# A two-layer graph network on one core: first layer's sums kept in SBUF, three PSUM banks of totals, a longer way out, and the second layer's way out in another order

## The chip, the cores and the metric

The kernel runs on one core of a Trainium2 chip. The metric is the device time of one execution in microseconds (us), the median over several runs. The engines are named as in the profile: PE (TensorE, matrix products), DVE (VectorE), ACT (ScalarE), POOL (GpSimd), SP (SyncE, which here only starts DMAs). SBUF is the on-chip memory, PSUM the banks into which PE writes.

## The reference

There are 6250 nodes with 256 features, 200000 edges sorted by their target `dst`, and 128 attributes on each edge. Two layers follow each other, each with a residual and a layer norm. Cut to what matters:

```python
# layer 1
e   = edge_attr @ W_edge + b_edge
msg = relu(x[src] + e)
agg = segment_sum(msg, dst, num_segments=N)
h   = (1.0 + eps) * x + agg
h   = relu(h @ W1 + b1) @ W2 + b2
h   = relu(batch_norm(h))             # mean and variance over the nodes
x   = layernorm(x + h)
# layer 2: four heads of 64
z   = einsum('nd,hdf->nhf', x, W)
e   = leaky_relu(es[src] + ed[dst])   # es, ed: z times the halves of att
ex  = exp(e - segment_max(e, dst)[dst])
out = segment_sum(ex / segment_sum(ex, dst)[dst] * z[src], dst)
x   = layernorm(x + out)
```

## The kernel before

The edges are cut into 1563 subtiles of 128. Fourteen subtiles make a group (112 groups), and two neighbouring subtiles make a pair (7 pairs in a group, 782 in all). The targets of a group's edges lie in a window of 128 nodes, so a segment sum over a group is a series of products with one-hot matrices, added up in one PSUM bank. A node whose edges run over a group's end gets a carry from one group to the next.

**Layer 1** takes from the start to about 2300 us. Its loop (from L728) runs over the pairs k. The steps are:

- `fetch(k+3)` (L645) issues on POOL two indirect DMAs, the gathers, each of 128 rows of x (with the edge bias added) by `src`, into a buffer `xg` (128x512, 11 buffers, in SBUF).
- `features(k+3)` (L653 and L655) multiplies on PE the edge attributes by W_edge into a PSUM bank `pt` (5 banks).
- `sums(k)` (L659, DVE) adds `xg` to `pt`, in `pt`; `xg` is free after it.
- `upper(k)` (L664, ACT) takes the relu of `pt`, rounded to the products' type, into one half of `hl`; `lower(k-1)` (L668, DVE) writes what the rounding lost, max(pt, 0) minus the upper half, into the other half. `pt` is free after it.
- `add_up(k-2)` (L678, PE) adds the pair into the group's bank `acc` by one-hots that ACT makes (L621, L627).

Four pairs after a group's last one, `flush` starts: `totals` adds the node's own x on DVE (L514, L515), transposes on PE (L518), copies on ACT (L520) and applies the carry on DVE (L523 to L531); for every second group `mlp` runs the two products for two groups (L408, L416; the relu r1 at L412 and the copy h2 at L424 on ACT), and `part_stats` (L431 to L440) adds to the batch norm's statistics. These are generators: a step yields the number of pairs to wait before its next step, and `drive` in the loop calls them.

**Between the layers**, from about 2300 to 2480 us, the batch norm, the residual, the layer norm and the tables of z are worked out.

**Layer 2** runs over groups i. POOL gathers 14 times 128 rows of z into `ring` (L1003; 70 places of one subtile, five groups). `places` (L1034, L1037, ACT) makes the transposed one-hots from `dlb`, which SP loads; PE takes from them the targets' part of the logits (L1054); `logits` (L1083 to L1087, then scans at L1072 and L1076) and `maxima` (L1119 to L1131) give the exponents on DVE and ACT; `weigh` multiplies them with the gathered z on DVE (y, L1140) and adds up on PE (acc, L1144) by one-hots of ACT (L1061, L1067). `carry` and `leave` take a group out: ACT copies the last group's carried row pc to pcs (L1151), DVE scales it (cr, L1153) and adds it to acc (L1155), ACT copies acc to ag (L1158), PE takes the next carried row from it (pc, L1160), and `finish_steps` (L371 to L389) divides, adds the residual and normalises; SP stores the result `o` (L1171).

The order of the work on DVE, PE, ACT and SP is the order in which the program lists it (a manual schedule); each engine works its list off in order and waits where an operand or a buffer is not ready. POOL's queue holds practically only the gathers, and it waits only for a free buffer. In `fetch` the wait is for a `xg` buffer, in layer 2 for a place of `ring`, which y frees.

Of the kernel before, what the change touches and what calls it, by code (L numbers as in the profile page):

```python
# [54 lines left out]
def gnn(ctx, tc, io, N, E):  # L55
# [345 lines left out]
    def mlp(hw, h2_dst, pool, pps, parts_=(None,)):  # L401

        w = len(parts_) * P
        p1 = pps.tile([P, 2, w], F32, tag="pt", name="p1")
        r1 = pool.tile([P, 2, w], F32, tag="r1", name="r1", bufs=1)
        for m in range(2):
            for k in range(2):
                nc.tensor.matmul(p1[:, m, :], w1_sb[:, k, m * P:(m + 1) * P], hw[:, k, :w],  # L408
                                 start=(k == 0), stop=(k == 1))
            yield 1 if m == 0 else 4  # L410
        for m in range(2):
            nc.scalar.activation(r1[:, m, :], p1[:, m, :], AF.Relu, bias=b1_c[:, m:m + 1])  # L412
        p2 = pps.tile([P, 2, w], F32, tag="pt", name="p2")
        for m in range(2):
            for k in range(2):
                nc.tensor.matmul(p2[:, m, :], w2_sb[:, k, m * P:(m + 1) * P], r1[:, k, :],  # L416
                                 start=(k == 0), stop=(k == 1))
            yield 1 if m == 0 else 4
        for i, part in enumerate(parts_):
            if i:  # L420
                yield 1
            cols_ = slice(i * P, (i + 1) * P)
            for m in range(2):
                nc.scalar.activation(h2_dst(m, i), p2[:, m, cols_], AF.Identity, bias=b2_c[:, m:m + 1])  # L424
            if part is not None:
                part(p2[:, :, cols_])
# [72 lines left out]
    with ExitStack() as st:  # L499
# [5 lines left out]
        pe = st.enter_context(tc.tile_pool(name="pe", bufs=5, space=PSUM))  # L505
        pg = st.enter_context(tc.tile_pool(name="pg", bufs=2, space=PSUM))
# [4 lines left out]
        def totals(g, acc, xw, hw):  # L511

            ag = wk.tile([P, D], F32, tag="ag", name="ag")
            nc.vector.scalar_tensor_tensor(ag, xw, opem[:, g:g + 1], acc[:, 1], op0=OP.mult, op1=OP.add)  # L514
            nc.vector.tensor_add(ag, ag, acc[:, 0])  # L515
            pT = acc[:, 0].rearrange("p (k n) -> p k n", k=2)
            for k in range(2):
                nc.tensor.transpose(pT[:, k, :], ag[:, k * P:(k + 1) * P], ident)  # L518
            yield 3
            nc.scalar.copy(hw, pT)  # L520
            old = carried[0]
            if old is not None:
                nc.vector.tensor_add(hw[:, :, 0], hw[:, :, 0], old)  # L523
            if g + 1 < G:
                end = nc.values_load(span_i[:1, g:g + 1], engines=[ET.DVE], min_val=0, max_val=P - 1,
                                     skip_runtime_bounds_check_because="the value is clamped")
                new = wk.tile([P, 2], F32, tag="carry", name="carry")
                nc.vector.tensor_scalar(new, pT[:, :, ds(end, 1)].rearrange("p k o -> p (k o)"), keep0[:, g:g + 1],  # L528
                                        None, op0=OP.mult)
                if old is not None:  # L530
                    nc.vector.scalar_tensor_tensor(new, old, whole0[:, g:g + 1], new, op0=OP.mult, op1=OP.add)  # L531
                carried[0] = new


        HW = {}

        def flush(g, acc, xw):

            two = G - G % 2 - 2
            if g < two and g % 2 == 0:  # L540
                HW[g + 1] = wk.tile([P, 2, 2 * P], F32, tag="hw", name="hw")
                yield from totals(g, acc, xw, HW[g + 1][:, :, :P])
                return
            hw = HW.pop(g, None)
            if hw is None:
                hw = wk.tile([P, 2, P], F32, tag="hw", name="hw1")
                yield from totals(g, acc, xw, hw)
                both = [g]
            else:
                yield from totals(g, acc, xw, hw[:, :, P:])  # L550
                both = [g - 1, g]
            yield -1
            bases = [nc.values_load(gf_i[:1, q:q + 1], engines=[ET.Activation], min_val=0, max_val=N - 1,
                                    skip_runtime_bounds_check_because=IN_RANGE) for q in both]
            yield from mlp(hw, lambda m, i: h2T[:, m, ds(bases[i], P)], wk, pps, [part_stats(q, wk) for q in both])
            if len(both) > 1:
                room[0] = 3
# [99 lines left out]
        def sums(k):  # L657
            g, j0, w = pairs_[k]
            nc.vector.tensor_add(PT[k][:, :w], PT[k][:, :w], XG.pop(k)[:, :w])  # L659

        def upper(k):
            g, j0, w = pairs_[k]
            HL[k] = hlp.tile([P, 2, 2, D], F32R, tag="hl", name="hl")
            nc.scalar.activation(HL[k][:, :w, 0], PT[k][:, :w], AF.Relu)  # L664

        def lower(k):
            g, j0, w = pairs_[k]
            nc.vector.scalar_tensor_tensor(HL[k][:, :w, 1], PT.pop(k)[:, :w], 0.0, HL[k][:, :w, 0].bitcast(F32),  # L668
# [17 lines left out]
        with tc.manual_schedule(engines={ET.DVE, ET.PE, ET.Activation, ET.SP}):  # L686
# [16 lines left out]
            hots, active, extras, room = iter(()), [], [], [0]  # L703
# [24 lines left out]
            for k in range(K + 2):  # L728
                g = pairs_[min(k, K - 1)][0]
                hurry = g >= G - 2  # L730
# [233 lines left out]
    with ExitStack() as st:  # L964
# [182 lines left out]
        def carry(g):  # L1147
            acc = T["acc", g]
            if g > 0:
                pcs = wk.tile([1, ZW], F32, tag="pcs", name="pcs")  # L1150
                nc.scalar.copy(pcs, T.pop(("pc", g - 1)))  # L1151
                cr = wk.tile([1, H, F + 1], F32, tag="cr", name="cr")
                nc.vector.tensor_tensor(cr, pcs.rearrange("p (h f) -> p h f", f=F + 1),  # L1153
                                        T.pop(("dm", g)).unsqueeze(2).to_broadcast([1, H, F + 1]), op=OP.mult)
                nc.vector.tensor_add(acc[:1], acc[:1], cr)  # L1155
            if g + 1 < G:
                ag = wk.tile([P, H, F + 1], F32, tag="ag2", name="ag2", bufs=2)
                nc.scalar.copy(ag, acc)  # L1158
                pc = T["pc", g] = ps.tile([1, ZW], F32, tag="pc", name="pc")
                nc.tensor.matmul(pc, ohlast[:, g:g + 1], ag.rearrange("p h f -> p (h f)"), start=True, stop=True)  # L1160

        def leave(g):
            px = rows_of(T.pop(("hw", g)), ps, "px")
            yield
            carry(g)
            o = wk.tile([P, D], F32, tag="o", name="o")
            yield from finish_steps(o, T.pop(("acc", g)), px, T.pop(("edw", g))[:, EW - 1:], wk)
# [33 lines left out]
        with tc.manual_schedule(engines={ET.DVE, ET.PE, ET.Activation, ET.SP}):  # L1201
# [10 lines left out]
            for i in range(G + 2):  # L1212
# [17 lines left out]
                if i + 1 < G:  # L1230
                    breaks(i + 1)
# [7 lines left out]
                if i == G - 1 and i > turn + 1:  # L1239
# [12 lines left out]
                    step(out)  # L1252
                    step(out)
# [3 lines left out]
                while out:  # L1257
                    step(out)
                step(outs)
                some(1, False)  # L1260
                step(spots)
                step(spots)
                for g in among([i - 1] if i <= turn else []):
                    rows_between(g)
                if i < G:
                    logits(i)
                some(1)
                step(hots)
# [4 lines left out]
                step(hots)  # L1273
                for g in among([i] if i >= turn else []):
                    rows_between(g)
                some(1)
# [3 lines left out]
                step(hots)  # L1280
                while outs:
                    step(outs)
                while units or hots:
                    some(1)
                    step(hots)
                for _ in parts_:
# [218 lines left out]
```

## Time and profile before

| | |
|---|---|
| median of 11 runs | 4953.35 us (4938.56 to 4963.66) |
| the profiled execution | 4952.23 us, span 4950.4 us |
| mean granted TensorE clock | 0.775 |
| busy: PE, DVE, ACT, POOL | 3059.7, 2699.4, 2632.4, 2968.1 us |
| gathers of layer 1: L645 | 1451 (and 112 from the first groups), mean 945 ns |
| gathers of layer 2: L1003 | 1563, mean 946 ns |
| `sums` L659, `upper` L664, `lower` L668 | 782 each, mean 691, 591, 679 ns |
| y L1140 | 782, mean 682 ns |
| 100 to 2000 us: PE, DVE, ACT, POOL busy | 1279.86, 1063.17, 1021.62, 1188.23 us |
| 2500 to 4800 us: PE, DVE, ACT, POOL busy | 1308.71, 1212.87, 1225.05, 1433.30 us |

The page gives for each group of instructions its line, engine, operation, the tiles written and read, the number, the total and mean duration, and the idle time of its engine just before it with what ended that idle time. "issue" means that the profile shows nothing that was waited for; "remote" means that the releaser is an event that the trace does not tie to an instruction. The operations of DVE and ACT are pipelined: the next one can start somewhat before the last one's end.

### The profile page before, as it was taken

The numbers are of one execution on the slowest core, as the hardware profiler recorded it, in microseconds if no ns is written. First come the engines' busy times: TensorE is split into PE (matmuls) and PEld (weight loads), VectorE is DVE, ScalarE is ACT, GpSimd is POOL, SyncE is SP. The second block draws the span as 40 slices with busy tenths as digits, with TensorE's granted clock in tenths as the row PEclk, the third lists the DMA queues.
The fourth block names the chain that finished last, engine by engine and source line by source line (L and its number), as shares of the span: only waits on it lengthen the run. The fifth ranks groups of instructions, "written<-read, shape, count | busy, mean of one in ns | idle before, by whom it ended". The sixth has DMA issues, their size and how long they took to land. (4 is left out here: it accounts for less than half of the span.)

```text
span 4950.4 us, 48894 instructions
## 1 busy us (share of the span) xinstructions
PE 3059.7 (62%) x11779; PEld 2181.6 (44%) x11779; DVE 2699.4 (55%) x7579; ACT 2632.4 (53%) x6723; POOL 2968.1 (60%) x3132
## 2 busy tenths in 40 slices
PE   6766666666666766666715655565656566555555
PEld 3545545555555555555603333333433333333343
DVE  5655555555555555555615555555555555555555
ACT  4555555555555555555525555555555555555554
POOL 7666566666666666666065666666666666666661
PEclk9888888888888888888857777777777767777777
DMA  7544444444444444444544444444444444444441
GB/s 255 163 140 139 130 137 141 139 139 140 130 139 137 142 137 140 139 140 131 154 128 115 122 126 125 120 125 126 122 117 127 126 122 126 119 124 126 128 122 42
DMA packets 296689, 656.22 MB, mean 133 GB/s; under 512 B 87274, under 2 KB 158553, under 8 KB 296394
## 3 DMA queue, kind: packets, MB, share of 16 engines
q0 software_dynamic: 150144, 416.54, 29.7%
q1 hardware_dynamic: 144650, 235.43, 14.9%
q8 instruction: 97, 1.59, 0.1%
q14 instruction: 198, 1.62, 0.1%
q10 hardware_dynamic: 1600, 1.04, 0.1%
HBM read 617.82 MB, written 34.99 MB: 132 GB/s over the span
## 5 line engine op out<-in xcount | busy, mean ns | idle before, releaser
L1003 POOL DMA_INDIRECT ring<-z_tab,src_sb x1563 | 1479.3, 946 | 1018.3 <-issue 422.0
L645 POOL DMA_INDIRECT xg<-xb_tab,src_sb x1451 | 1371.8, 945 | 822.3 <-DVE pt L659 409.6
L1144 PE MATMUL acc<-y,oh 128*128 128x260 f32 x3126 | 1173.1, 512 | 451.2 <-issue 333.8
L655 PE MATMUL pt<-we_sb,ea_t 128*128 128x256 f32 x3126 | 967.7, 439 | 244.1 <-DVE hl L668 203.6
L1144 PEld LDWEIGHTS acc<-y,oh 128*128 128x128 f32 x3126 | 701.1, 247 | 704.4 <-issue 416.6
L664 ACT ACTIVATE hl<-pt 128x512 fp32r<-128x512 f32 x782 | 462.4, 591 | 948.8 <-DVE pt L659 823.0
L659 DVE TENSOR_TENSOR pt<-pt,xg 128x512 f32<-128x512 f32 x782 | 540.5, 691 | 645.3 <-remote 534.5
L655 PEld LDWEIGHTS pt<-we_sb,ea_t 128*128 128x128 f32 x3126 | 662.2, 220 | 423.7 <-issue 262.5
L678 PE MATMUL acc<-hl,oh 128*128 128x512 f32 x1563 | 720.3, 544 | 35.8 <-DVE carry L528 17.6
L1140 DVE TENSOR_TENSOR y<-ring,exs 128x520 f32<-128x520 f32 x782 | 514.5, 682 | 60.5 <-issue 23.3
L668 DVE SCALAR_TENSOR_TENSOR hl<-pt,hl 128x512 fp32r<-128x512 f32 x782 | 530.7, 679 | 2.2 <-issue 0.9
L621 ACT ACTIVATE oh<-consts,dloc 128x128 fp32r<-128x128 f32 x1549 | 508.5, 394 | 0.0
L1061 ACT ACTIVATE oh<-consts,dloc 128x128 f32<-128x128 f32 x1563 | 480.4, 388 | 0.7 <-remote 0.7
L1034 ACT ACTIVATE ohT<-dlb,niota 128x1792 bf16<-128x1792 bf16 x112 | 199.7, 1783 | 354.9 <-DMA dlb<-dl_tab 173.7
L678 PEld LDWEIGHTS acc<-hl,oh 128*128 128x128 f32 x1563 | 339.4, 219 | 107.7 <-issue 39.3
L416 PE MATMUL p<-r,w_sb 128*128 128x256 f32 (+1 forms) x456 | 162.7, 491 | 286.3 <-ACT r L412 267.1
L1054 PEld LDWEIGHTS <-ohT 128*128 128x128 bf16 x1563 | 159.1, 113 | 357.3 <-issue 273.6
L1054 PE MATMUL pds<-edw,ohT 128*128 128x12 bf16 x1563 | 155.3, 177 | 190.6 <-issue 166.7
L416 PEld LDWEIGHTS p<-r,w_sb 128*128 128x128 f32 x456 | 108.7, 252 | 326.3 <-ACT r L412 283.5
L1153 DVE TENSOR_TENSOR cr<-pcs,dm 1x260 f32<-1x260 f32 x111 | 46.6, 419 | 374.8 <-ACT pcs L1151 189.2
L1067 ACT ACTIVATE oh<-oh 128x896 f32<-128x896 f32 x224 | 208.7, 932 | 7.8 <-remote 7.8
L627 ACT ACTIVATE oh<-oh 128x896 fp32r<-128x896 f32 (+1 forms) x222 | 209.1, 942 | 0.0
(226 smaller groups left out, 3086.1 us busy)
## 6 DMA issues: line engine op xcount, KB each, us to landing
ea_t<-in_eaT SPq DMA_DIRECT2D x110, 896.0 KB
dlb<-dl_tab SPq DMA_DIRECT2D x111, 448.0 KB
ring<-z_tab,src_sb POOLq DMA_INDIRECT x1563
xg<-xb_tab,src_sb POOLq DMA_INDIRECT x1451
xw<-in_x SPq DMA_DIRECT2D x112, 128.0 KB
hw<-hT_tab SPq DMA_DIRECT2D x112, 128.0 KB
out<-o SPq DMA_DIRECT2D x110, 128.0 KB
z_tab<-zt SPq DMA_DIRECT2D x11, 528.0 KB
```

Source lines behind the costliest of these rows:

```text
L621: nc.scalar.activation(oh[:, i], iota_r, AF.Square, bias=dloc[:, gs[g] + i:gs[g] + i + 1], scale=-1.0)
L645: nc.gpsimd.indirect_dma_start(out=XG[k][:, i, :], out_offset=None, in_=io["x"] if g < GB else xb_tab, in_offset=bass.IndirectOffsetOnAxis ...
L655: nc.tensor.matmul(pt[:, i, :], EA.pop(gs[g] + j0 + i), we_sb, start=not g < GB, stop=(not g < GB or i == w - 1))
L659: nc.vector.tensor_add(PT[k][:, :w], PT[k][:, :w], XG.pop(k)[:, :w])
L664: nc.scalar.activation(HL[k][:, :w, 0], PT[k][:, :w], AF.Relu)
L668: nc.vector.scalar_tensor_tensor(HL[k][:, :w, 1], PT.pop(k)[:, :w], 0.0, HL[k][:, :w, 0].bitcast(F32), op0=OP.max, op1=OP.subtract)
L678: nc.tensor.matmul(ACC[g].rearrange("p a d -> p (a d)"), OH[g][:, j0 + i], hl[:, i].rearrange("p a d -> p (a d)"), start=(j0 + i == 0), st ...
L1003: nc.gpsimd.indirect_dma_start(out=zg[:, j, :], out_offset=None, in_=z_tab, in_offset=bass.IndirectOffsetOnAxis(ap=src_sb[:, t:t + 1], axi ...
L1054: nc.tensor.matmul(pd[:, j].rearrange("p h c -> p (h c)"), ohT[:, j * P:(j + 1) * P], T["edw", g].bitcast(BF16)[:, :3 * H], start=True, st ...
L1061: nc.scalar.activation(oh[:, i], iota_r, AF.Square, bias=dloc[:, gs[g] + i:gs[g] + i + 1], scale=-1.0)
L1140: nc.vector.tensor_tensor(y[:, :w], T["zg", g][:, j0:j0 + w, :ZW].rearrange("p s (h f) -> p s h f", f=F + 1), by_edge(T["ex", g], g)[:, j0 ...
L1144: nc.tensor.matmul(T["acc", g].rearrange("p h f -> p (h f)"), T["oh", g][:, j0 + i, :], y[:, i].rearrange("p h f -> p (h f)"), start=(j0 + ...
```

## The change

In words:

- `sums` writes its result into `xg` (SBUF) instead of `pt` (PSUM). `pt` is free after `sums`, and `xg` only after `lower`. `upper` and `lower` read `xg`.
- There are 4 banks of products (`pe`) instead of 5, and 3 banks of totals (`pg`) instead of 2.
- In `totals` three pairs lie between DVE's sum and PE's transposes, four before ACT's copy and one before the carry. In `mlp` three pairs lie between the first product's relu and the second product, and the statistics come one pair after the copies, each part one pair after the other.
- Layer 2's `leave` holds the whole way out: ACT copies the carried row and then acc as PE has left it; the carry that goes through a group is added on DVE with one more operation (L1166 in the changed file), then cr and the sum; the next carried row is taken from the copy. `breaks`, `rows_between`, `places` and `logits` have other places in the iteration.

In the changed file `fetch` is at L648, `sums` at L662, `lower` at L671, y at L1143, the sum of acc and cr at L1170.

```diff
--- before.py
+++ after.py
@@ -398,7 +398,7 @@
     cs = list(zip(cuts, cuts[1:]))
     stat = stage.enter_context(tc.tile_pool(name="stat", bufs=1))
 
-    def mlp(hw, h2_dst, pool, pps, parts_=(None,)):
+    def mlp(hw, h2_dst, pool, pps, parts_=(None,), room=None):
 
         w = len(parts_) * P
         p1 = pps.tile([P, 2, w], F32, tag="pt", name="p1")
@@ -407,23 +407,25 @@
             for k in range(2):
                 nc.tensor.matmul(p1[:, m, :], w1_sb[:, k, m * P:(m + 1) * P], hw[:, k, :w],
                                  start=(k == 0), stop=(k == 1))
-            yield 1 if m == 0 else 4
+            yield 1 if m == 0 else 3
         for m in range(2):
             nc.scalar.activation(r1[:, m, :], p1[:, m, :], AF.Relu, bias=b1_c[:, m:m + 1])
+        if room and not room[1] and len(parts_) > 1:
+            room[0] = 3
+        yield 3
         p2 = pps.tile([P, 2, w], F32, tag="pt", name="p2")
         for m in range(2):
             for k in range(2):
                 nc.tensor.matmul(p2[:, m, :], w2_sb[:, k, m * P:(m + 1) * P], r1[:, k, :],
                                  start=(k == 0), stop=(k == 1))
-            yield 1 if m == 0 else 4
+            yield 1 if m == 0 else 3
         for i, part in enumerate(parts_):
-            if i:
+            for m in range(2):
+                nc.scalar.activation(h2_dst(m, i), p2[:, m, i * P:(i + 1) * P], AF.Identity, bias=b2_c[:, m:m + 1])
+        for i, part in enumerate(parts_):
+            if part is not None:
                 yield 1
-            cols_ = slice(i * P, (i + 1) * P)
-            for m in range(2):
-                nc.scalar.activation(h2_dst(m, i), p2[:, m, cols_], AF.Identity, bias=b2_c[:, m:m + 1])
-            if part is not None:
-                part(p2[:, :, cols_])
+                part(p2[:, :, i * P:(i + 1) * P])
 
     def part_stats(g, pool):
         def part(p2):
@@ -502,8 +504,8 @@
         wk = st.enter_context(tc.tile_pool(name="wk", bufs=2))
         hlp = st.enter_context(tc.tile_pool(name="hlp", bufs=6))
         ohp = st.enter_context(tc.tile_pool(name="ohp", bufs=3))
-        pe = st.enter_context(tc.tile_pool(name="pe", bufs=5, space=PSUM))
-        pg = st.enter_context(tc.tile_pool(name="pg", bufs=2, space=PSUM))
+        pe = st.enter_context(tc.tile_pool(name="pe", bufs=4, space=PSUM))
+        pg = st.enter_context(tc.tile_pool(name="pg", bufs=3, space=PSUM))
         pps = st.enter_context(tc.tile_pool(name="pps", bufs=1, space=PSUM))
         carried = [None]
         wide = pen_f.shape[1] >= TB * D
@@ -513,11 +515,13 @@
             ag = wk.tile([P, D], F32, tag="ag", name="ag")
             nc.vector.scalar_tensor_tensor(ag, xw, opem[:, g:g + 1], acc[:, 1], op0=OP.mult, op1=OP.add)
             nc.vector.tensor_add(ag, ag, acc[:, 0])
+            yield 3
             pT = acc[:, 0].rearrange("p (k n) -> p k n", k=2)
             for k in range(2):
                 nc.tensor.transpose(pT[:, k, :], ag[:, k * P:(k + 1) * P], ident)
-            yield 3
+            yield 4
             nc.scalar.copy(hw, pT)
+            yield 1
             old = carried[0]
             if old is not None:
                 nc.vector.tensor_add(hw[:, :, 0], hw[:, :, 0], old)
@@ -533,6 +537,7 @@
 
 
         HW = {}
+        room = [0, False]
 
         def flush(g, acc, xw):
 
@@ -549,12 +554,10 @@
             else:
                 yield from totals(g, acc, xw, hw[:, :, P:])
                 both = [g - 1, g]
-            yield -1
+            yield -3
             bases = [nc.values_load(gf_i[:1, q:q + 1], engines=[ET.Activation], min_val=0, max_val=N - 1,
                                     skip_runtime_bounds_check_because=IN_RANGE) for q in both]
-            yield from mlp(hw, lambda m, i: h2T[:, m, ds(bases[i], P)], wk, pps, [part_stats(q, wk) for q in both])
-            if len(both) > 1:
-                room[0] = 3
+            yield from mlp(hw, lambda m, i: h2T[:, m, ds(bases[i], P)], wk, pps, [part_stats(q, wk) for q in both], room)
 
         def window(g):
             base = nc.values_load(gf_i[:1, g:g + 1], engines=[ET.SP], min_val=0,
@@ -656,16 +659,16 @@
 
         def sums(k):
             g, j0, w = pairs_[k]
-            nc.vector.tensor_add(PT[k][:, :w], PT[k][:, :w], XG.pop(k)[:, :w])
+            nc.vector.tensor_add(XG[k][:, :w], PT.pop(k)[:, :w], XG[k][:, :w])
 
         def upper(k):
             g, j0, w = pairs_[k]
             HL[k] = hlp.tile([P, 2, 2, D], F32R, tag="hl", name="hl")
-            nc.scalar.activation(HL[k][:, :w, 0], PT[k][:, :w], AF.Relu)
+            nc.scalar.activation(HL[k][:, :w, 0], XG[k][:, :w], AF.Relu)
 
         def lower(k):
             g, j0, w = pairs_[k]
-            nc.vector.scalar_tensor_tensor(HL[k][:, :w, 1], PT.pop(k)[:, :w], 0.0, HL[k][:, :w, 0].bitcast(F32),
+            nc.vector.scalar_tensor_tensor(HL[k][:, :w, 1], XG.pop(k)[:, :w], 0.0, HL[k][:, :w, 0].bitcast(F32),
                                            op0=OP.max, op1=OP.subtract)
 
         def add_up(k):
@@ -700,7 +703,7 @@
             side = [positions(r, ldp) for r in range(1, len(parts))]
             rest = [first_table()]
             checks = [order(r, ldp) for r in range(len(parts))]
-            hots, active, extras, room = iter(()), [], [], [0]
+            hots, active, extras = iter(()), [], []
             fill = zeros()
             for f in range(min(LOOK, K)):
                 fetch(f)
@@ -727,7 +730,7 @@
 
             for k in range(K + 2):
                 g = pairs_[min(k, K - 1)][0]
-                hurry = g >= G - 2
+                hurry = room[1] = g >= G - 3
                 if k < K and pairs_[k][1] == 0:
                     hots = hot(g + 1) if g + 1 < G else iter(())
                     if g + 2 < G:
@@ -1144,27 +1147,39 @@
                 nc.tensor.matmul(T["acc", g].rearrange("p h f -> p (h f)"), T["oh", g][:, j0 + i, :],
                                  y[:, i].rearrange("p h f -> p (h f)"), start=(j0 + i == 0), stop=(j0 + i == n - 1))
 
-        def carry(g):
+        def leave(g):
+
+
             acc = T["acc", g]
+            px = rows_of(T.pop(("hw", g)), ps, "px")
             if g > 0:
                 pcs = wk.tile([1, ZW], F32, tag="pcs", name="pcs")
                 nc.scalar.copy(pcs, T.pop(("pc", g - 1)))
+            yield
+            if g + 1 < G:
+                ag = wk.tile([P, H, F + 1], F32, tag="ag2", name="ag2", bufs=2)
+                nc.scalar.copy(ag, acc)
+            yield
+            if g > 0:
                 cr = wk.tile([1, H, F + 1], F32, tag="cr", name="cr")
+                if g > 1:
+                    nc.vector.scalar_tensor_tensor(pcs, T.pop(("cr", g - 1)).rearrange("p h f -> p (h f)"),
+                                                   whole0[:1, g - 1:g], pcs, op0=OP.mult, op1=OP.add)
                 nc.vector.tensor_tensor(cr, pcs.rearrange("p (h f) -> p h f", f=F + 1),
                                         T.pop(("dm", g)).unsqueeze(2).to_broadcast([1, H, F + 1]), op=OP.mult)
                 nc.vector.tensor_add(acc[:1], acc[:1], cr)
+                T["cr", g] = cr
+            o = wk.tile([P, D], F32, tag="o", name="o")
+            steps = finish_steps(o, T.pop(("acc", g)), px, T.pop(("edw", g))[:, EW - 1:], wk)
+            next(steps)
+            yield
             if g + 1 < G:
-                ag = wk.tile([P, H, F + 1], F32, tag="ag2", name="ag2", bufs=2)
-                nc.scalar.copy(ag, acc)
                 pc = T["pc", g] = ps.tile([1, ZW], F32, tag="pc", name="pc")
                 nc.tensor.matmul(pc, ohlast[:, g:g + 1], ag.rearrange("p h f -> p (h f)"), start=True, stop=True)
-
-        def leave(g):
-            px = rows_of(T.pop(("hw", g)), ps, "px")
+            next(steps)
             yield
-            carry(g)
-            o = wk.tile([P, D], F32, tag="o", name="o")
-            yield from finish_steps(o, T.pop(("acc", g)), px, T.pop(("edw", g))[:, EW - 1:], wk)
+            for _ in steps:
+                pass
             if g + KT < G:
                 obase = nc.values_load(gout[:1, g:g + 1], engines=[ET.SP], min_val=0, max_val=N - P,
                                        skip_runtime_bounds_check_because="the value is a minimum with the bound")
@@ -1227,8 +1242,6 @@
                     maxima(g)
                 if i + 2 < G:
                     parts_ = dst_parts(i + 2)
-                if i + 1 < G:
-                    breaks(i + 1)
 
                 def some(k, parts=True):
                     for _ in range(min(k, len(units))):
@@ -1249,40 +1262,47 @@
                         step(hots)
                     logits(i)
                     out = [leave(g) for g in work]
-                    step(out)
-                    step(out)
+                    for _ in range(3):
+                        step(out)
                     rows_between(i)
                     step(out)
                     continue
                 while out:
                     step(out)
+                if i + 1 < G:
+                    breaks(i + 1)
                 step(outs)
-                some(1, False)
-                step(spots)
-                step(spots)
                 for g in among([i - 1] if i <= turn else []):
                     rows_between(g)
+                step(spots)
+                some(1, False)
                 if i < G:
                     logits(i)
-                some(1)
-                step(hots)
+                step(spots)
                 some(1)
                 step(hots)
                 some(1)
                 step(outs)
                 step(hots)
+                some(1)
+                step(hots)
                 for g in among([i] if i >= turn else []):
                     rows_between(g)
+                step(outs)
                 some(1)
                 step(hots)
                 step(outs)
                 some(1)
                 step(hots)
+                some(1)
                 while outs:
                     step(outs)
                 while units or hots:
                     some(1)
                     step(hots)
+                    if len(work) > 1 and not out and len(units) < 4 and ("acc", work[0]) in T:
+                        out = [leave(work[0])]
+                    step(out)
                 for _ in parts_:
                     pass
 
```

## The prediction

> **What bounds the kernel now.** I read the engine totals first, then the groups, the waits, and the timeline of a few cycles. The profiled execution took 4952.23 us (span 4950.4, 1.8 around it), 0.02% under the median 4953.35, so a sum made on it stands for the median. About 0.2% (10 us) is what a measurement of this kernel can tell from no change.
>
> ```profile
> PE 3059.7 (62%) x11779; PEld 2181.6 (44%) x11779; DVE 2699.4 (55%) x7579; ACT 2632.4 (53%) x6723; POOL 2968.1 (60%) x3132
> L645 POOL DMA_INDIRECT xg<-xb_tab,src_sb x1451 | 1371.8, 945 | 822.3 <-DVE pt L659 409.6
> L659 DVE TENSOR_TENSOR pt<-pt,xg 128x512 f32<-128x512 f32 x782 | 540.5, 691 | 645.3 <-remote 534.5
> ```
>
> No engine is full. POOL only gathers, 945 ns each, and starts one every 1.25 us when it is free: 17.5 us for a group of 14. The windows give 1256 gathers in 100 to 2000 us and 1515 in 2500 to 4800, so 1.513 and 1.518 us each: 21.2 us per group in both layers, or 3.7 us of stops per group. The waits say for whom POOL stops (total us, times, longest):
>
> ```profile
> DVE pt L659 <- remote: 534.5, 95, 10.8
> POOL xg L645 <- DVE pt L659: 426.2, 175, 5.6
> POOL ring L1003 <- DVE y L1140: 369.8, 133, 15.4
> PEld p L416 <- ACT r L412: 283.5, 38, 9.6
> ACT ag L1158 <- DVE acc L1155: 246.1, 79, 11.3
> PE pt L655 <- DVE hl L668: 203.6, 65, 9.5
> ```
>
> The timeline of one cycle of layer 1, POOL's rows and then DVE's (start, length, instruction, idle before):
>
> ```profile
> 1409.81 0.95 POOL L645 DMA_INDIRECT xg<-xb_tab,src_sb  x1 [0.30 <-issue]
> 1414.31 0.94 POOL L645 DMA_INDIRECT xg<-xb_tab,src_sb  x1 [3.55 <-DVE pt L659]
> ```
> ```profile
> 1413.34 0.70 DVE L659 TENSOR_TENSOR pt<-pt,xg 128x512 f32<-128x512 f32 x1 [2.28 <-remote]
> 1413.95 0.68 DVE L668 SCALAR_TENSOR_TENSOR hl<-pt,hl 128x512 fp32r<-128x512 f32 x1
> 1414.55 0.69 DVE L659 TENSOR_TENSOR pt<-pt,xg 128x512 f32<-128x512 f32 x1
> ```
>
> From 1393.56 to 1409.81 POOL issued 14 gathers without a gap, then its 11 pair buffers were full. DVE's L659 waits on PE's semaphore; PE had done the products, but its signals reached DVE 2.6 us after POOL's last gather, five within 0.3 us. The trace does not name the cause; over 100 to 2300 us, 502 of L659's signals come late like this and 243 in time. So a cycle is: seven pairs of gathers, 2.6 us, the first sums (0.7), 0.27 to POOL's restart.
>
> **The change: sums on SBUF.** L659 now writes into the gathered buffer, so `upper` and `lower` read it there, and `lower` (L668) frees it instead of L659. First cost: DVE's order is sums(k), lower(k-1), so a full POOL waits for the lower behind the sums as well. The rows above put them 0.60 us apart: a stop of 3.7 becomes 4.3. Second cost: `lower` used to read one operand in PSUM and one in SBUF; now both lie in SBUF. The nearest row with both there is L1153:
>
> ```profile
> 3573.32 0.42 DVE L1153 TENSOR_TENSOR cr<-pcs,dm 1x260 f32<-1x260 f32 x1 [1.49 <-ACT pcs L1151]
> 3573.39 1.17 POOL L1003 DMA_INDIRECT ring<-z_tab,src_sb  x1 [0.30 <-issue]
> ```
>
> The gather that starts 70 ns into it takes 1.17 us instead of 0.95. Gathers that start later in L1153 lose less (1052 ns when 190 ns in, 951 at 292), and one that starts 76 ns into L587 (1024 elements, both in SBUF) takes 1970. So the gather waits until some 297 ns of the 260-element operation and 1101 ns of the 1024-element one have passed; in proportion, 562 ns for 512 elements. A SCALAR_TENSOR_TENSOR does it too: L1085, 56 elements, makes gathers of 979 and 984. Under L668 as it is now, with one input in PSUM, gathers keep 945. I laid the 782 lowers of this trace over its gathers: 391 gathers start between 42 and 562 ns into one, with 76 us left to wait in all. That goes on the path, since POOL paces. Bounds: 0, if the stretched gathers only fill the stops; 124, if the whole 680 ns blocks (the same overlay). I take 76.
>
> The Trainium skill ("SBUF — State Buffer", "Who interferes with whom") says that a DVE instruction with two SBUF inputs contends with a GpSimd instruction that reads SBUF, and that the first to start holds the port for its whole instruction. The rows agree on the contention but not on the whole: L1153 lets go 120 ns before its end. By the rule the term would be 124 and the forecast 5066.
>
> **What layer 1 gains.** The PSUM banks of products go from 5 to 4, but each is now freed by sums(k) and not by lower(k): the product of k+3 waits for sums(k-1) instead of lower(k-2), which stands just behind it on DVE. So the look-ahead stays and PE restarts 0.6 us earlier in each cycle. The waits of L416 for r1 (283.5) and of L518 for ag go, since both now have three pairs of products ahead of them; so does most of DVE's wait for h2 (136.0). None of these is the releaser of POOL; what they buy is more pairs signalled in time per cycle. PE spends about 2.9 us on a pair (four L655 at 0.44, two L678 at 0.54, their share of the rest); 0.6 us earlier and half of the 2.4 us per cycle of L416's wait make 1.8/2.9 = 0.6 pair at best, nothing at worst. At 7 pairs a cycle is 17.5 + 4.3 = 21.8 us, 3.11 per pair against 3.03 now, +67 us over 782 pairs; at 7.4 pairs (18.5 + 4.3)/7.4 = 3.08, +40; at 8 pairs 3.04, +7. I take 7.4: **+40**, bounds 7 and 67.
>
> `upper` reads SBUF now: by the rows of 128 (394 ns, L621) and 896 elements (942, L627) 512 would take about 0.67 instead of 0.59. It lies beside lower(k-1) on DVE (0.60 us pace), and ACT has 949 us of idle time before it: 0; without that cover 0.08 x 782 = 60. The third bank of totals takes away 17.6 us of PE waits that release nobody: 0. The longer way out of the MLP delays only the next group's statistics, which nothing in the loop reads: 0.
>
> **Layer 2.** ACT's copy of acc (L1158) stood behind DVE's cr (0.42) and acc (0.42), which stood behind ACT's pcs; after it come the one-hots that the next group's y products need. Now ACT copies acc as soon as PE has it, and DVE adds the carry afterwards, with one more operation of 1x260 (0.42 x 110) ahead of its finishing steps. A typical place in the timeline, ACT's rows and then DVE's:
>
> ```profile
> 3615.96 0.36 ACT L1151 COPY pcs<-pc 1x260 f32<-1x260 f32 x1 [1.20 <-remote]
> 3620.09 0.38 ACT L1158 COPY ag<-acc 128x260 f32<-128x260 f32 x1 [3.77 <-DVE acc L1155]
> ```
> ```profile
> 3616.35 0.42 DVE L1153 TENSOR_TENSOR cr<-pcs,dm 1x260 f32<-1x260 f32 x1 [6.97 <-issue]
> 3619.63 0.42 DVE L1155 TENSOR_TENSOR acc<-acc,cr 1x260 f32<-1x260 f32 x1 [2.86 <-remote]
> ```
>
> Here PE's signal comes last, at 3619.63; the new order starts ag 0.46 us earlier and leaves DVE's finish where it was. Where ACT's pcs is what holds DVE (189 us in 51 waits), cr and pcs go too, 1.2 us in all. The new waits: DVE's acc (L1170) waits for ag, with rd, fin and the next y behind it; ag is 0.38 us, so those start no later than today; `breaks` moves past the leave on ACT, beside a wait. `rows_between` and logits swap with y's on DVE at equal counts. SP's and POOL's queues get the same DMAs. A group has 3.7 us above POOL's 17.5, so a shorter loop can pay, at most 1.2 us x 111 = 133; at least 0, if the same late signals set the stop; below that, 0.42 x 110 = 46 lost if DVE's finish is last. I take 0.46 x 111 = **-50**, by the row shown.
>
> **Sum.** 4952 + 76 + 40 - 50 = 5018 us.
>
> **Rivals.** (1) Faster. Layer 1's PE, rid of its waits, gets 8 pairs into each cycle (+7), half of the port waits falls on gathers that POOL would have waited after anyway (+38), and layer 2 wins the whole 1.2 us per group (-133): 4864. For it speak 267 us of PE idle behind L412 and 246 of ACT behind acc; against it that the late signals, and not these waits, are what POOL waits for. It decides from the point where layer 2 gains over 1 us per group. Chance 0.27. (2) Much slower: PE's freedom buys no pair (+67), the port costs 76, and the late signals give layer 2 nothing: 5095. Chance 0.20. (3) The parts cancel: 8 pairs, +7, port +76, layer 2 -0.75 x 111 = -83: 4952. Nearly the same, 4942, comes out if the contention does not occur for `lower`, whose output has another type than L1153's. L438, also with two inputs in SBUF, stretched one gather only; but only two started in its first 42 to 163 ns: one took 1052, the other held up L438 itself, 392 ns for 346. Chance 0.07 together.
>
> **How the numbers follow.** The forecast has 0.46; its own range is 4980 to 5066, from half the port waits (38) to the port held for the whole lower (124). Faster: 0.27, all rival 1. Same: most of the 0.07 of rival 3, 0.06. Slower: 0.67. For 8 in 10 the range reaches to just above rival 1's price and beyond rival 2's by 20 us for uncovered ACT: 4870 to 5115.
>
> **What would show it.** In the profile after: a mean of L648's gathers near 0.99 to 1.0 us with maxima near 1.5, against 945 ns; POOL's waits named after `lower` (L671) and not sums, near 4.2 us; no wait of L416 for r; ag waiting for PE instead of DVE; layer 1 to about 2415 us instead of 2300, layer 2 shorter by 50. It is wrong if gathers stay at 945 ns, if POOL's waits in layer 1 sum to under the 426 us of now, or if layer 2 changes by more than 133 us.

## The result and the profile after

The changed kernel takes 5002.91 us (median of 8 runs, 4996.79 to 5008.77) against 4954.68 (31 runs): the ratio is 1.0097, with a 95% interval of 1.0085 to 1.0108, so it is slower by 48 us. The profiled execution took 4999.51 us, span 4997.6.

The same kernel before takes about 4955 us on some chips and about 4118 us on others, so each run below is compared with the kernel before on its own chip, and the text says which kind it was ("late" chips at 4955 us, "prompt" chips at 4118 us, for a reason given with the experiments; the first chip, of the forecast and of the result, is a late one).

The groups of the profile after, POOL's gathers and the sums (line, engine, operation, count, busy us, mean ns, idle before):

```profile
L1006 POOL DMA_INDIRECT ring<-z_tab,src_sb x1563 | 1479.9, 947 | 1071.1 <-issue 379.3
L648 POOL DMA_INDIRECT xg<-xb_tab,src_sb x1451 | 1417.1, 977 | 777.9 <-issue 357.8
L662 DVE TENSOR_TENSOR xg<-pt,xg 128x512 f32<-128x512 f32 x782 | 533.9, 683 | 943.3 <-remote 717.3
```

Layer 1's gathers now take 977 ns instead of 945; layer 2's are as before. The waits after (total us, times, longest):

```profile
DVE xg L662 <- remote: 717.3, 110, 10.8
DVE acc L1170 <- ACT ag L1161: 324.3, 57, 16.0
POOL ring L1006 <- DVE y L1143: 273.5, 95, 11.5
POOL ring L1006 <- DVE e L1086: 221.5, 34, 16.0
POOL xg L648 <- DVE hl L671: 184.6, 115, 5.4
ACT pcs L1157 <- remote: 151.3, 12, 19.9
```

POOL in layer 1 waits for `lower` (hl L671), by the profile's names also for two operations of the way out on DVE (mk L433 110.7 us, carry L532 76.6 us); waits named after the sums are down from 426.2 to 42.6 us. The wait of L416 (now L419) for r, 283.5 us before, is down to 5.5 us. ACT's pcs now waits 151.3 us for late signals, where it waited 40.4. The windows after, one of layer 1 and one of layer 2 (PE, PEld, DVE, ACT and POOL busy with their counts, clock, DMA share, GB/s):

```profile
100.00:2000.00 1900.00, 1295.01 (x4731) 984.49 (x4731) 1069.04 (x2530) 1046.03 (x2794) 1229.46 (x1257) 0.81 0.45 141
2550.00:4850.00 2300.00, 1303.30 (x5176) 831.08 (x5176) 1234.07 (x3926) 1190.11 (x2902) 1390.42 (x1469) 0.69 0.44 119
```

In layer 1 POOL is busy 41 us longer, and yet it issues 1257 gathers in the 1900 us, where it issued 1256. In layer 2 it issues 1469 in 2300 us, where it issued 1515 (in the same length, 50 us earlier). Counted in POOL's timeline:

| us | before | after |
|---|---|---|
| start of layer 1's last gather | 2359.7 | 2363.7 |
| layer 1's gathers, what is over 946 ns, summed | 9.8 | 54.7 |
| layer 1's stops of POOL over 0.8 us (but for its first start), summed | 438.2 in 154 | 393.7 in 142 |
| layer 2, first to last gather | 2368.5 | 2428.3 |
| from the last gather to the end | 93.2 | 82.9 |

So layer 1 breaks even (+4 us), the loop of layer 2 loses 60, and the end wins 10.

What the forecast calls port contention can be read in single rows of the timeline after, DVE's and then POOL's (start, length):

```profile
1219.67 0.68 DVE L671 SCALAR_TENSOR_TENSOR hl<-xg,hl 128x512 fp32r<-128x512 f32 x1
1222.58 0.68 DVE L671 SCALAR_TENSOR_TENSOR hl<-xg,hl 128x512 fp32r<-128x512 f32 x1
```
```profile
1218.54 0.95 POOL L648 DMA_INDIRECT xg<-xb_tab,src_sb  x1 [0.31 <-DVE g_mean L438]
1219.80 1.38 POOL L648 DMA_INDIRECT xg<-xb_tab,src_sb  x1 [0.30 <-issue]
1221.47 0.94 POOL L648 DMA_INDIRECT xg<-xb_tab,src_sb  x1 [0.30 <-issue]
1222.72 1.35 POOL L648 DMA_INDIRECT xg<-xb_tab,src_sb  x1 [0.30 <-issue]
```

The gathers that start 130 and 140 ns into a lower take 1.38 and 1.35 us; their neighbours 0.95. Over the whole trace 190 gathers start 42 to 562 ns into a lower and wait 45.7 us in all. Before, 391 did so and none was stretched.

### The profile page after: what moved, and what is told of

Same layout as the page of the kernel before. It is cut to its first block, busy times and chain, and to the rows that moved or that the text cites. A ratio compares the mean times of both kernels' runs of the same rounds, so it can differ in the third digit from the quotient of the medians.

```text
span 4997.6 us, 49057 instructions
## 1 busy us (share of the span) xinstructions
PE 3079.0 (62%) x11779; PEld 2167.8 (43%) x11779; DVE 2736.6 (55%) x7689; ACT 2640.1 (53%) x6723; POOL 3014.2 (60%) x3132
## 5 line engine op out<-in xcount | busy, mean ns | idle before, releaser
L648 POOL DMA_INDIRECT xg<-xb_tab,src_sb x1451 | 1417.1, 977 | 777.9 <-issue 357.8
L658 PE MATMUL pt<-we_sb,ea_t 128*128 128x256 f32 x3126 | 1001.0, 447 | 521.9 <-DVE xg L662 439.0
L1147 PEld LDWEIGHTS acc<-y,oh 128*128 128x128 f32 x3126 | 686.6, 241 | 921.4 <-issue 525.7
L662 DVE TENSOR_TENSOR xg<-pt,xg 128x512 f32<-128x512 f32 x782 | 533.9, 683 | 943.3 <-remote 717.3
L667 ACT ACTIVATE hl<-xg 128x512 fp32r<-128x512 f32 x782 | 488.5, 625 | 809.6 <-DVE xg L662 688.6
L671 DVE SCALAR_TENSOR_TENSOR hl<-xg,hl 128x512 fp32r<-128x512 f32 x782 | 531.8, 680 | 6.7 <-ACT hl L667 2.5
L1143 DVE TENSOR_TENSOR y<-ring,exs 128x520 f32<-128x520 f32 x782 | 503.4, 679 | 27.8 <-remote 22.2
L681 PEld LDWEIGHTS acc<-hl,oh 128*128 128x128 f32 x1563 | 343.1, 220 | 120.5 <-issue 58.8
L1170 DVE TENSOR_TENSOR acc<-acc,cr 1x260 f32<-1x260 f32 x111 | 47.1, 425 | 395.8 <-ACT ag L1161 324.3
L1157 ACT COPY pcs<-pc 1x260 f32<-1x260 f32 x111 | 40.1, 362 | 374.6 <-remote 151.3
L1040 ACT ACTIVATE ohT<-ohT 128x1792 bf16<-128x1792 bf16 x112 | 189.5, 1692 | 3.6
```

Source lines behind the costliest of these rows:

```text
L648: nc.gpsimd.indirect_dma_start(out=XG[k][:, i, :], out_offset=None, in_=io["x"] if g < GB else xb_tab, in_offset=bass.IndirectOffsetOnAxis ...
L658: nc.tensor.matmul(pt[:, i, :], EA.pop(gs[g] + j0 + i), we_sb, start=not g < GB, stop=(not g < GB or i == w - 1))
L662: nc.vector.tensor_add(XG[k][:, :w], PT.pop(k)[:, :w], XG[k][:, :w])
L667: nc.scalar.activation(HL[k][:, :w, 0], XG[k][:, :w], AF.Relu)
L671: nc.vector.scalar_tensor_tensor(HL[k][:, :w, 1], XG.pop(k)[:, :w], 0.0, HL[k][:, :w, 0].bitcast(F32), op0=OP.max, op1=OP.subtract)
L681: nc.tensor.matmul(ACC[g].rearrange("p a d -> p (a d)"), OH[g][:, j0 + i], hl[:, i].rearrange("p a d -> p (a d)"), start=(j0 + i == 0), st ...
```

## The experiments

My theory after the result: the port costs what the rows say, the longer way out pays for it in layer 1, and the order of layer 2 is what loses. Rivals: the earlier release of the product's bank pays, or layer 1 loses and layer 2 wins, and the first chip only hides it.

**Layer 1 alone, layer 2 alone.** The hunks of the diff up to the loop of layer 1, or those of layer 2, on the kernel before.

> Layer 1 of the changed kernel with layer 2 of before. The traces of before and after put the last gather of layer 1 at 2359 and 2363 us, so layer 1 looks paid for: theory (the loss is all in layer 2): 4955 to 4962 us, gathers of layer 1 near 977 ns. Rival (layer 1's and layer 2's costs are tied, for example by the state in which layer 1 leaves the queues): 4970 us or more.

> Layer 1 of before with layer 2 of the changed kernel. Theory (the loss is all in layer 2, whose gathers came 60 us later at the end): 5000 to 5010 us, gathers of both layers at 946 ns. Rival (layer 2's order alone gains, as forecast, and the loss is from layer 1): 4905 us.

Both came out against the first theory, on a chip where the kernel before takes 4117.29 us: layer 1 alone 4221.35 (ratio 1.0252, 1.0238 to 1.0266), so +104; layer 2 alone 4081.01 (0.9911, 0.9896 to 0.9926), so -36. Two waits of layer 2 alone (whose layer 1 is that of before) show what is different there:

```profile
DVE pt L659 <- DMA xg<-xb_tab,src_sb: 228.7, 145, 4.5
POOL xg L645 <- DVE pt L659: 51.2, 168, 0.3
```

The sums wait for gathered data, not for a late signal of PE ("remote", 534.5 us, in the first profile), and POOL never waits longer than the 0.3 us that lie between any two gathers. PE's signals come in time. So POOL runs through at 1.25 us per gather, and what stretches a gather is paid in full:

```profile
L648 POOL DMA_INDIRECT xg<-xb_tab,src_sb x1451 | 1480.5, 1020 | 442.1 <-issue 281.8 <-DVE xg L662 84.1 <-DMA xg<-xb_tab,src_sb 31.1
```

This is layer 1 alone: 1020 ns instead of 946; its gathers are 118.8 us over 946 ns against 9.1, and the time is 104 longer.

**The two parts of layer 1.** Either only the sums in SBUF (and 4 banks of products),

```diff
-            nc.vector.tensor_add(PT[k][:, :w], PT[k][:, :w], XG.pop(k)[:, :w])
+            nc.vector.tensor_add(XG[k][:, :w], PT.pop(k)[:, :w], XG[k][:, :w])
```

with upper and lower reading `XG`, or only the way out, the banks (4 and 3) and the sums left in PSUM.

> Only the sums in SBUF, in the kernel before (4 banks of products, 2 of totals, way out as before). Theory (port contention and the later release of the buffers cost, and only the longer way out pays for it): gathers of layer 1 near 977 ns (+46 us), stops near 4.2 us, 7 pairs per cycle, 5030 to 5075 us. Rival (freeing the product's bank at the sums is what pays): 4950 to 4970 us with 16 to 18 gathers between stops.

> Only the three banks of totals, four banks of products and the longer way out in layer 1; the sums stay in PSUM, so a bank of products is freed by lower. Theory (the way out gives the longer cycles): 4900 to 4930 us, gathers at 945 ns and more than 14 gathers between stops; if the bank that is missing cuts the look-ahead from four pairs to three, shorter cycles and 4980 to 5050 us. Rival (the way out does nothing for layer 1): 4950 us, stops as before.

On the same chip: the sums 4183.71 (1.0156, 1.0142 to 1.0170), gathers of 988 ns; the way out 4117.09 (1.0001, 0.9992 to 1.0010). There the way out does nothing, since POOL has no stops that it could shorten, and the fourth bank was not missed. The sums cost 66 us, and their gathers are 74.4 us over 946 ns, 65 more than in layer 2 alone. The two together (layer 1 alone) cost 104 and not 66. With the way out, DVE has less to wait for and runs at the heels of the gathers:

```profile
DVE xg L662 <- DMA xg<-xb_tab,src_sb: 610.3, 344, 4.8
```

is a row of layer 1 alone, against 262.1 us in 168 waits with the sums alone. A lower that starts when data has landed keeps step with POOL: 391 gathers start 42 to 562 ns into a lower in layer 1 alone, 229 with the sums alone. That the step is what raises the count is argued from these rows, not tried by itself.

**Is it the second SBUF input?** As the sums alone, but lower's second input is a bank of zeros in PSUM. This kernel leaves out the remainder of the rounding, and its lower no longer waits for ACT's upper half:

```diff
-            nc.vector.scalar_tensor_tensor(HL[k][:, :w, 1], XG.pop(k)[:, :w], 0.0, HL[k][:, :w, 0].bitcast(F32),
+            nc.vector.scalar_tensor_tensor(HL[k][:, :w, 1], XG.pop(k)[:, :w], 0.0, nilp[:, :w],
```

> As sbuf_only (sums in SBUF, four banks of products, two of totals), but the second input of lower is a bank of zeros in PSUM instead of the upper half in SBUF, so that lower computes max(sum, 0) and not the remainder: the operation, its length and its output stay, one of its two SBUF inputs goes. Theory (DVE's two SBUF inputs hold up the gathers): gathers of layer 1 back at 946 ns, and on a chip with signals in time the time of before within 10 us (4117); rival (the sums' way through SBUF costs in another way, by the later release of the buffers): near sbuf_only's ratio, 1.016.

4119.87 us against 4117.41 (1.0005, 0.9996 to 1.0014):

```profile
L648 POOL DMA_INDIRECT xg<-xb_tab,src_sb x1451 | 1372.8, 946 | 442.0 <-issue 240.7 <-DVE hl L671 32.6 <-ACT hl L667 28.6
```

The same operation with one input in SBUF leaves the gathers at 946 ns, and the whole price is gone, though the buffers are still released by lower. That lower no longer waits for ACT does not explain it: 327 gathers still start 42 to 562 ns into a lower, and together they run 0.1 us over 946 ns. This settles the mechanism.

**Do the halves add?** The changed kernel itself, and layer 2 with ACT's copy pcs moved:

```diff
-            if g > 0:
-                pcs = wk.tile([1, ZW], F32, tag="pcs", name="pcs")
-                nc.scalar.copy(pcs, T.pop(("pc", g - 1)))
             yield
+            if g > 0:
+                pcs = wk.tile([1, ZW], F32, tag="pcs", name="pcs")
+                nc.scalar.copy(pcs, T.pop(("pc", g - 1)))
             if g + 1 < G:
```

> The changed kernel, run beside others on one chip. If the chip is one on which PE's signals come in time (before at 4117 us), the two halves measured there, +104 us for layer 1 alone and -36 us for layer 2 alone, should add: theory 4185 us; rival (the halves are tied, as their sum of +68 against the +48 of the first chip could mean) 4165 us or less. If the chip is one on which they come late (before near 4955 us): 5003 us again, with layer 1's gathers at 977 ns and fewer stops.

> Layer 1 of before, layer 2 of the changed kernel, but ACT copies the carried row (pcs) only just before acc, behind the one-hots, as in before. On a chip with late signals: theory (pcs at the head of ACT's list waits for PE's late signal and holds up the one-hots) 4900 to 4960 us where layer 2 of the changed kernel costs 60; rival (the loss has another source) 5000 us or more. On a chip with signals in time, where pcs has long been ready: within 10 us of l2_only (ratio 0.991).

Again on a prompt chip (before 4117.41): the changed kernel 4180.16 (1.0151, 1.0137 to 1.0165), +63 where the halves sum to +68. Layer 2 with pcs late 4074.11 (0.9895, 0.9880 to 0.9911): better than both kernels there.

Nearly all of the 36 us of layer 2 lie after the last gather on these chips. From the first to the last gather of layer 2 the way out alone (layer 2 as before) takes 1966.8 us and layer 2 alone 1962.3, both POOL's pace; from there to the end 79.4 and 44.7. With the old order four groups' exponents (exs) are still to come when the last gather starts, with the new one two. So the other engines run further ahead in layer 2, as a shorter loop would have it, but POOL hides that until its own work ends. Whether it comes from the earlier copy of acc, as forecast, or from the order, no run on such a chip tells apart. The first of the two last stores, which POOL issues:

```profile
4093.93 1.00 POOL L1176 DMA_INDIRECT out<-o,oidx  x1 [56.55 <-ACT pcs L1154]
4056.13 1.00 POOL L1185 DMA_INDIRECT out<-o,oidx  x1 [21.05 <-ACT pcs L1154]
```

The first row is of the way out alone, the second of layer 2 alone: POOL waits 35 us less for it.

**The same questions where the signals come late.** The sums back in PSUM in the changed kernel; pcs late in the changed kernel; and only the order of layer 2's iteration.

> The changed kernel with the sums back in PSUM (the three edits of sums, upper and lower undone; four banks of products, three of totals, the longer way out and layer 2 stay). Theory (all of layer 1's price is the port): on a chip with signals in time 4081 us (ratio 0.991), gathers at 946 ns; rival (the price is the release of buffers with the longer way out) 4150 or more. On a chip with late signals (before at 4955): theory (the longer way out pays 46 us there and the port takes it back) 4955 us; rival (way out pays nothing) 5003.

> The changed kernel, with ACT's copy of the carried row (pcs) put back behind the one-hots, just before the copy of acc. On a chip with signals in time: 4174 us, 7 under the changed kernel, as in layer 2 alone. On a chip with late signals: theory (pcs at the head of ACT's list is layer 2's loss) 4940 to 4970 us; rival 4995 to 5010.

> The kernel before with only the other order of layer 2's iteration (breaks, rows_between, places, logits and the early way out of the last groups), the way out of a group itself as before: its carry still goes from DVE's acc to ACT's ag to PE and on to the next group. On a chip with signals in time: theory (the 35 us that layer 2 wins after the last gather come from the carry that no longer runs through the groups one by one) 4117 us, 80 us from the last gather to the end; rival (they come from the early way out of the last groups) 4081 us, 45 us after the last gather.

This chip was a late one (before 4957.77). Sums in PSUM: 4979.35 (1.0040, 1.0022 to 1.0058). pcs late: 4977.78 (1.0040, 1.0027 to 1.0053). Both lie between the theory's figure and the rival's, so each theory holds in part only. Order alone: 4997.24 (1.0076, 1.0052 to 1.0099). From their traces:

| us | last gather of layer 1 | layer 2, first to last gather | after the last gather |
|---|---|---|---|
| before | 2359.7 | 2368.5 | 93.2 |
| order only | 2371.3 | 2415.4 | 84.3 |
| changed, sums in PSUM | 2337.8 | 2431.3 | 82.9 |
| changed | 2363.7 | 2428.3 | 82.9 |
| changed, pcs late | 2363.6 | 2411.6 | 83.8 |

The first two rows have the same layer 1, so single profiles differ by 12 us in it. The way out wins 22 to 34 us in layer 1; the sums in SBUF take 26 back. The order of layer 2 alone costs 47 in its loop (39 of the whole time by the medians), and it alone brings 9 of the 10 us that the end wins; pcs at the head of ACT's list costs another 17. The rest of the new way out, ACT's earlier copy of acc with it, is worth the 4 us between order only and pcs late, less than single profiles differ. A place where pcs costs, ACT's rows in the profile after:

```profile
3638.69 0.18 ACT L1046 COPY brk<-negs 128x1 f32<-128x1 f32 x1
3650.18 0.36 ACT L1157 COPY pcs<-pc 1x260 f32<-1x260 f32 x1 [11.30 <-PE acc L1147]
3650.45 0.18 ACT L1111 COPY down<-down 4x1 f32<-4x1 f32 x1
3650.54 1.78 ACT L1037 ACTIVATE ohT<-dlb,niota 128x1792 bf16<-128x1792 bf16 x1
```

pcs waits 11.30 us for PE, and the transposed one-hots, which need nothing of it, stand behind it. What in the order costs the 47 us is narrowed by the waits of the order alone, against those of before, both from 2600 to 4700 us:

```profile
DVE top L1119 <- remote: 211.3, 26, 36.0
ACT exs L1126 <- DVE v L1124: 197.9, 66, 31.0
```

Before these were 85.0 and 86.3 us: the maxima now meet PE's late signal. One stop of POOL in the order alone, DVE's rows and then POOL's, shows what stands behind them:

```profile
2749.53 0.17 DVE L1119 TENSOR_TENSOR top<-top,trbk 128x8 f32<-128x8 f32 x1 [7.50 <-remote]
2751.64 0.68 DVE L1140 TENSOR_TENSOR y<-ring,exs 128x520 f32<-128x520 f32 x1
2752.25 0.32 DVE L1083 TENSOR_REDUCE e<-pds 128x56 f32<-128x168 f32 x1
```
```profile
2752.59 0.94 POOL L1003 DMA_INDIRECT ring<-z_tab,src_sb  x1 [5.26 <-DVE e L1083]
```

POOL's waits that end like this, after e of the logits, are 120.5 us in 20 from 2600 to 4700 us, and were 0.3; those after y fell from 348.2 to 239.6. That the late signal is met because of the order is argued from these rows; which of its moves does it was not tried by itself on a late chip.

**Two versions that could be better.** Sums in PSUM with the longer way out, and on it either layer 2 of the change with pcs late and the first y ahead again, or layer 2 of before with only the last hunk of the diff:

```diff
                 step(outs)
+                some(1, False)
                 for g in among([i - 1] if i <= turn else []):
                     rows_between(g)
                 step(spots)
-                some(1, False)
```

> Sums in PSUM, the longer way out, layer 2 of the changed kernel with pcs copied behind the one-hots and with the first y of an iteration back at its place ahead of rows_between and of the first places. On a chip with late signals (before near 4955): theory (the y that comes later is what the other order of layer 2 costs, 47 us between its first and last gather) way out -22, tail -10, order 0: 4925 us, ratio 0.994; rival (the order costs in another place, the maxima's wait for PE) 4955 to 4970. On a chip with signals in time: 4074 us, ratio 0.990, whichever holds.

> Sums in PSUM, the longer way out, and layer 2 of before but for the last hunk of the diff (in the iteration that has two groups to add up, the first of them leaves early). On a chip with late signals: -22 from the way out and, if that hunk is what shortens the time after the last gather, -10: 4925 us; without it 4933. On a chip with signals in time: theory (the hunk is what shortens the time after the last gather from 80 to 45 us) 4082 us; rival (the rest of the order or of leave does) 4117 us.

A prompt chip again (before 4120.82): 4083.48 (0.9906, 0.9891 to 0.9921) and 4121.44 (1.0001, 0.9992 to 1.0010). The last hunk does not shorten the end (80.3 us). For the first y on a late chip the run says nothing, so that question stays open; neither version was run on a late chip.

## Why the prediction was right, and where two of its terms were not

The direction, the range (4870 to 5115) and nearly the size (5018 against 5003) came out. By its terms, on the first chip, it was less good than that. Of its own signs, the longer gathers (977 ns, where it had 0.99 to 1.0 us), waits named after `lower` and stops of over 4 us were seen; that POOL's waits in layer 1 would not fall below those of before, that layer 1 would end later by some 100 us and layer 2 be shorter by 50 were not: the stops fell from 438.2 to 393.7 us, layer 1's last gather came 4 us later, and layer 2 grew longer.

- *The port, +76.* The mechanism is shown by the run with the second input in PSUM. The size depends on how the lowers lie to the gathers: 45 us on the first chip, where 190 gathers fell on a lower and not the 391 of the overlay, and 65 to 112 on prompt chips. The law from two rows, that a gather waits until 562 ns of the lower have passed, holds: one that starts 71 ns into it takes 1432 ns (946 + 486), one at 539 takes 952. The Trainium skill ("SBUF — State Buffer", "Who interferes with whom") has the contention right for this operation too. That the port is held for the whole instruction, which the same page says of two SBUF inputs under "SBUF: two separate sides", does not fit here: the gathers get it before the lower's 680 ns are over, and the measurement decides.
- *Longer stops against more pairs per cycle, +40.* Here a term had the wrong sign. Single stops did become longer: 52 lie between 4 and 5 us, where before 79 lay between 3 and 4. But before, 69 stops came after a run of exactly 14 gathers; now 61 come after 16 to 20, eight to ten pairs, where the forecast had allowed 7.4 pairs, and the sum of the stops falls from 438.2 to 393.7 us. The changed kernel with the sums in PSUM tells two effects apart. It too has lost the wait behind L416, and its stops of 1 to 3 us are down from 67 to 21 and their sum from 438.2 to 403.2 us (order only, with layer 1 of before, has 73 and 455.9); yet 91 of its 121 stops still come after exactly 14 gathers. So the way out does away with short stops, and the longer runs belong to the sums in SBUF and not to L416's wait. The forecast had a step for it (the product waits for the sums "instead of lower(k-2)") and priced it at 0.6 us per cycle, too low. That this bank, freed earlier, is what lengthens the runs is argued, not tried by itself, from PE's waits for a free bank with the sums in PSUM and in the changed kernel:

```profile
PE pt L658 <- DVE hl L671: 605.1, 148, 9.2
PE pt L658 <- DVE xg L662: 439.0, 154, 9.7
```

- *Layer 2, -50.* On the first chip the loop lost 60 and the end won 10. The step that failed is "`rows_between` and logits swap with y's on DVE at equal counts", priced at nothing: that swap with its neighbours (breaks, places and the early way out of the last groups) costs 47. And the forecast has no price for pcs ahead of the one-hots on ACT's list, which costs 17. Its own gain, 0.46 us per group from the earlier copy of acc, cannot be seen: 4 us in the loop. On prompt chips layer 2 wins 36, at the end only.
- On the first chip the wrong signs of two terms cancel, which was luck: by the trace layer 1 gives +4, the tables between the layers -6, the loop +60 and the end -10, together 48, where the forecast had 76 + 40 - 50 = 66. The sum was right for reasons that were half wrong. On prompt chips, which the profile before did not show, the two halves add: +104 - 36 = +68, measured +63; POOL has no stops there, so the forecast's +40 has no counterpart.
- *Rival 1* had its way with layer 1's cycles but not with layer 2. *Rival 4942*, that the contention does not occur for lower's output type, is refuted.

## What to carry to other kernels

An operand moved from PSUM to SBUF can cost an engine that does not read it: where POOL's DMA issue is the pace, look for DVE instructions with two SBUF inputs, and overlay their durations on the gathers of the trace to price it. An instruction that waits for a late event belongs as far back in its engine's list as its consumers allow, for everything behind it waits too. A gain in a loop that another engine paces may show only where that engine's work ends.

## What was not expected of the hardware

The same kernel differs by 20% between chips (4955 against 4118 us). On the slower ones PE's signals reach DVE late while POOL issues gathers: in the first profile 502 of 745 signals on the semaphore of L659 from 100 to 2300 us, some 300 of them 2.5 to 3 us after POOL's last gather; in the nine profiles from the others none in that stretch. The granted TensorE clock is lower there as well (0.775 in the first profile, 0.835 to 0.845 for the kernel before on the others). Why the signals are late, and whether the clock has to do with it, was not found, and no run tried to change it. So a schedule tuned on one kind of chip need not be the better on the other: layer 2's new order wins 36 us on the one and loses some 50 on the other.
